# Additions of a tile and scatters of a step left unordered among themselves; the input's load taken in the preceding step, routing and norms spread over turns

## The chip, the core and the metric

The kernel runs on one core of a Trainium2 chip. The core has five engines that run side by side and wait for one another through semaphores: PE (TensorE, matrix products), DVE (VectorE), ACT (ScalarE), POOL (GpSimd) and SP (SyncE, which here only issues transfers). In the traces an engine starts its instructions in the order in which they stand in its stream, so one that waits holds up all behind it. Transfers are carried out by 16 DMA engines shared by all queues. The metric is device microseconds of the one core; lower is better.

## The reference, cut to what matters

Two layers work on an image batch x of 2 x 56 x 56 x 256 numbers in float32 (6272 tokens of 256 channels).

```python
# layer 0: neighborhood attention, window 7 x 7, 8 heads
x = x + L0_conv(_gn(x), ...)
# layer 1: linear attention with a gate and a running sum over tokens
t = x.reshape(B, 3136, 256)
t = t + L1_attn(_ln_t(t), ...)
# layer 1: a mixture of 8 experts, each token goes to its best two
probs = softmax(_ln_t(t) @ gate_w + gate_b)
top2_vals, top2_idx = top_k(probs, 2)
cw = zeros.at[token, top2_idx].add(top2_vals)
for e in range(8):
    t += cw[:, e] * (gelu(xf @ W1[e] + b1[e]) @ W2[e] + b2[e])
```

All of it is computed in float32. The attention of layer 1 carries sums from token to token, so it goes through the tokens in order. The experts need only a token's normalized value, its two experts and their weights.

## The kernel before, in words

**Layer 0** (up to about 485 us) is not touched by the change. It leaves its result in device memory (`x1_d`).

**Layer 1** is the function `layer_1`, run with `general` false. It cuts the tokens into 14 steps of 448 tokens (224 of each of the two images), held as four pieces of 112 tokens. The work of a step is written as Python generators that `yield` at the end of each turn:

- `before_pairs(s)` (from line 725) loads the step's input `x_acc` (line 729), normalizes and transposes it (`norm_T`, lines 690 to 722), projects it to q, k and v (line 749), and makes the gates and the softmax's running maxima and sums. Between norm and projection it adds the output bias `bo1` to x (line 737).
- `attention(s)` makes the running sums (`sums_plain`, lines 867 to 965) and adds the projected result to x (line 981).
- `route(s)` stores x into `out` (line 1151), normalizes and transposes it into `xs` (`norm_T` again), makes the gate's softmax, ranks the experts and gives each token its two slots (`rowi`, line 1249). It then writes each token's row twice into `xs_d`, a buffer in device memory that has a region for every expert: eight indirect transfers from POOL, one for each piece of 112 tokens and each of the two slots (the scatters, line 1253). `listed(s)` writes down which blocks of 256 slots are full by now.
- `experts()` goes through 56 tiles of 256 slots. `fetch` reads a tile's rows from `xs_d` into `xg` (line 1361) and the expert's weights into `wj` (line 1365), two tiles ahead of their use, both issued by SP. `gather` transposes `xg` on PE, `hidden` makes the first product and the gelu (lines 1389 and 1396), `results` reads the token numbers out of `xg` (`rows_e`, a cast on DVE, line 1404), starts `ye` from the second bias (ACT, line 1421), makes the second product (line 1426), adds it to `ye` (DVE, line 1433) and adds `ye` to the tokens' rows in `out`: one indirect transfer from POOL, with addition, for each half of 128 rows (the additions, line 1436).

`together` advances these generators side by side: `attention(s)` is the main one, and `route(s - 1)`, `before_pairs(s + 1)` and the tiles of experts get their turns in proportion. Each gets a stretch of the main one in which it is to run:

```python
with_it.append((route(s - 1), n_route, 0, 0.6))
with_it.append((before_pairs(s + 1), n_before, 0, 1))
with_it.append((tiles, n_tiles * per_tile + (begin > 0), 0.5 if begin else 0, 1))
```

The last four tiles sure to be full run beside `route` of the last step, and the other 14 alone at the end.

The order that is traced in this way is the priority of a scheduler, which then fixes the order of each engine's stream and places every wait. It works from the accesses to each buffer: two instructions that write the same buffer are ordered by a wait for the earlier one. `xs_d` and `out` are one buffer each to it, whatever rows an indirect transfer touches. So each scatter waits until the scatter before it has landed, each addition until the addition before it has landed, each read of `xs_d` (line 1361) until the last scatter traced before it has landed, and a scatter also until reads of `xs_d` traced before it are done.

Rows of a tile that no token fills come from `empty`, whose token number points behind the 6272 rows of `out`, into 128 rows that nobody reads.

Of the kernel before, what the change touches and what calls it, by code (L numbers as in the profile page):

```python
# [14 lines left out]
F32 = mybir.dt.float32  # L15
# [3 lines left out]
ALU = mybir.AluOpType  # L19
# [4 lines left out]
P = 128  # L24
NB = 2
IMG = 56
L = IMG * IMG
C = 256
# [12 lines left out]
TT = 112  # L41
BLK = 448
BT = BLK // NB
NST = L // BT
# [41 lines left out]
def constants():  # L86

    c = {}
    c["gavg"] = np.kron(np.eye(P // 8), np.full((8, 8), 1 / 8)).astype(np.float32)

    ind = np.zeros((P, NG, NB, 16), np.float32)
    for g in range(NG):
        for b in range(NB):
            for p in range(P):
                ind[p, g, b, b * NH + g * 4 + p // HD] = 1
    c["ind"] = ind.reshape(P, -1)
    c["rep"] = np.ascontiguousarray(ind.transpose(3, 1, 2, 0)).reshape(16, -1)
# [12 lines left out]

    e2 = np.repeat(e, 2).astype(np.float32)
    i2 = np.tile(np.arange(2), NE).astype(np.float32)
    cand = np.concatenate([(e2 - NE) * RG + i2 * SL, e2, i2, i2 + 1, np.arange(NX) + 1, e])
    c["cand"] = np.ascontiguousarray(np.broadcast_to(cand.astype(np.float32), (P, cand.size)))

    empty = np.zeros((P, ROW), np.float32)
    empty[:, TOK] = NB * L + np.arange(P)
    c["empty"] = np.tile(empty, (1, SL // P))
# [35 lines left out]
def hybrid_kernel(ctx: ExitStack, tc: tile.TileContext, t: dict, out: bass.AP):  # L154
# [7 lines left out]
    xs_d = dram.tile([NE * RG + SL, ROW], F32, name="xs_d")  # L162
    ident = const.tile([P, P], F32, name="ident")
    make_identity(nc, ident)

    def load(pool, name, shape, src, eng=None, dt=F32):
        dst = pool.tile(shape, dt, name=name)
# [469 lines left out]
    def layer_1(general):  # L637
        with (
# [51 lines left out]
            def norm_T(x, tag, pool, xn=None):  # L690

                st = p2.tile([TT, NTI, 6], F32, tag="lst", name="lst")
                mv = p2.tile([TT, NTI, 2], F32, tag="lmv", name="lmv")
                for i in range(NTI):
                    nc.vector.bn_stats(st[:, i, :], x[:, i, :])
                    nc.vector.bn_aggr(mv[:, i, :], st[:, i, :])
                rs = p2.tile([TT, NTI], F32, tag="lrs", name="lrs")
                nc.vector.tensor_scalar_add(rs, mv[:, :, 1], LN_EPS)
                nc.scalar.activation(rs, rs, AF.Sqrt)
                nc.vector.reciprocal(rs, rs)  # L700
                xT = pool.tile([P, NG, BLK], F32, tag=tag, name=tag)
                if xn is None:
                    xn = p1.tile([TT, NTI, C], F32, tag="xn", name="xn")
                yield
                for i in range(NTI):
                    nc.vector.tensor_scalar(  # L706
                        xn[:, i, :C],
                        x[:, i, :],
                        mv[:, i, 0:1],
                        rs[:, i : i + 1],  # L710
                        ALU.subtract,
                        ALU.mult,
                    )
                for g in range(NG):
                    pt = ps_m.tile([P, NTI, TT], F32, tag="mm", name="pt_x")
                    for i in range(NTI):
                        nc.tensor.transpose(  # L717
                            pt[:, i, :], xn[:, i, g * P : (g + 1) * P], ident[:TT, :TT]
                        )
                    nc.scalar.copy(xT[:, g, :], pt.rearrange("p i t -> p (i t)"))  # L720
                    yield
                return xT

            def before_pairs(s):
# [3 lines left out]
                for b in range(NB):  # L728
# [5 lines left out]
                    )  # L734
                yield
                xT = yield from norm_T(x, "xT_a", p1)
                nc.vector.tensor_tensor(
                    x, x, bo1.unsqueeze(1).to_broadcast([TT, NTI, C]), ALU.add
                )
# [27 lines left out]
                for g in range(NG):  # L767
                    ps = ps_m.tile([P, BLK], F32, tag="mm", name="p_u")
                    nc.tensor.matmul(
                        ps,  # L770
                        lhsT=wbd[:, g].rearrange("p h e -> p (h e)"),
                        rhs=v[:, g, :],
                        start=True,
                        stop=True,
                    )
                    nc.vector.tensor_tensor(pd[:, 3, g, :], ps, k[:, g, :], ALU.mult)
                    yield
                ps = ps_m.tile([P, BT], F32, tag="mm", name="p_sum")
                at = 0
                for g in range(NG):  # L780
# [186 lines left out]
            def attention(s):  # L967
                x, q, k, v, gl, cf = ready.pop(s)
                yield from (sums_general if general else sums_plain)(s, q, k, v, gl, cf)

                for i in range(NTI):
                    ps = ps_m.tile([TT, C], F32, tag="mm", name="p_out")
# [173 lines left out]
            def route(s):  # L1146
# [1 line left out]
                nonlocal n_prev, c_prev, at_prev  # L1148
                x = routed.pop(s)
                for b in range(NB):  # L1150
                    nc.gpsimd.dma_start(
                        out=out[b * L + s * BT : b * L + (s + 1) * BT].rearrange(
                            "(i p) e -> p i e", p=TT
                        ),
                        in_=x[:, b * 2 : (b + 1) * 2, :],
                    )
                xs = p3.tile([TT, NTI, ROW], F32, tag="xs", name="xs")
                nc.gpsimd.memset(xs[:, :, CWC + NE :], 0.0)
# [89 lines left out]
                rowi = p2.tile([TT, 2, NTI], I32, tag="rowi", name="rowi")  # L1248
                nc.vector.tensor_scalar_add(rowi, rows, float(NE * RG))
                yield  # L1250
                for i in range(NTI):
                    for c in range(2):
                        nc.gpsimd.indirect_dma_start(  # L1253
                            out=xs_d[:, :],
                            out_offset=bass.IndirectOffsetOnAxis(
                                ap=rowi[:, c, i : i + 1].bitcast(U32), axis=0
                            ),
                            in_=xs[:, i, :],
                            in_offset=None,
                        )  # L1260
                    yield
                listed(s)
                yield

# [77 lines left out]
            def fetch(j):  # L1342
# [18 lines left out]
                nc.sync.dma_start(  # L1361
                    out=xg, in_=xs_d[bass.ds(row, SL), :].rearrange("(u p) c -> p u c", p=P)
                )
                wj = p3.tile([P, NG * FF + NF * C + NF + C], F32, tag="wj", name="wj")
                nc.sync.dma_start(
                    out=wj, in_=t["we"][bass.ds(exp, 1)].rearrange("o p c -> (o p) c")
# [33 lines left out]
            def results(j, hT, xg, wj):  # L1400
# [18 lines left out]
                for u in range(SL // P):  # L1419
                    y = p6.tile([P, C], F32, tag="ye", name="ye")  # L1420
                    nc.scalar.activation(y, b2, AF.Copy, scale=cws[:, u : u + 1])  # L1421
                    ys.append(y)
                for u, y in enumerate(ys):
                    py = ps_h.tile([P, C], F32, tag="mm", name="p_y")
                    for f in range(NF):
# [10 lines left out]
                    nc.gpsimd.indirect_dma_start(  # L1436
                        out=out[:, :],
                        out_offset=bass.IndirectOffsetOnAxis(
                            ap=rows[:, u : u + 1].bitcast(U32), axis=0
# [2 lines left out]
                        in_offset=None,  # L1442
                        compute_op=ALU.add,
                    )
                    yield

            def experts():

# [39 lines left out]


            ready, routed, listed_at = {}, {}, {}  # L1490
            ahead = 1 if general else 2
            wait = 1 if general else 4
            tiles = experts()
            per_tile = NF + 1 + SL // P
            n_before = sum(1 for _ in before_pairs(0)) + 1
            n_step, n_route = 45, 13
            for s in range(NST):
                n_tiles = max(0, sure(s - 1) - wait) - max(0, sure(s - 2) - wait)
                begin = n_tiles and sure(s - 2) <= wait
                with_it = []  # L1500
                if s and not general:
                    with_it.append((route(s - 1), n_route, 0, 0.6))
                if s + 1 < NST:
# [88 lines left out]
```

## Time and profile before

| | |
|---|---|
| time, median of 3 runs | 1746.69 us (1733.62 to 1760.24) |
| span of the profiled execution | 1705.8 us |
| PE busy | 1400.5 us (82%) |
| DVE busy | 921.0 us (54%) |
| ACT busy | 703.9 us (41%) |
| POOL busy | 449.8 us (26%) |
| scatters (line 1253) | 112, 953 ns on POOL each, 2.6 us from issue to landing |
| additions (line 1436) | 112, 1585 ns on POOL each, 3.9 us from issue to landing |

The profile is of one execution; its span is shorter than the median time. PE is busy 82% of the span, but a matmul counts as busy from its start to its modelled end, and at a lower clock each takes longer. The stretches are: layer 0 to 485 us, steps without expert tiles to about 730 us, steps with them to about 1450 us, then tiles alone. In the views below, "who waited for whom" gives the total, the number of times and the longest wait; in a timeline, the columns are the start in us, the duration in us, engine, line, operation and tiles, and in square brackets the idle time before and what ended it.

### The profile page before, as it was taken

To read this page: it belongs to the slowest core of one execution; us is meant where nothing else is said; L and a number is where in the kernel's file an instruction comes from. 1 tells how busy PE (TensorE), PEld (TensorE's weight loads), DVE (VectorE), ACT (ScalarE), POOL (GpSimd) and SP (SyncE) were. 2 spreads that over 40 slices of the span, in tenths; PEclk is the share of its full clock that TensorE was granted. 3 is DMA by queue.
4 is the path that set the end of the run, shared out by engine and by line. 5 is a ranking of instruction groups with operands and counts; after the bars stand their busy time and mean duration, and the time that the engine had idled before them with its cause. 6 is when DMAs were issued, how large, how long until landed. Compare 5 with 4: busy or idle time off the path is not lost. (4 is left out here: it accounts for less than half of the span.)

```text
span 1705.8 us, 28462 instructions
## 1 busy us (share of the span) xinstructions
PE 1400.5 (82%) x10672; PEld 1022.5 (60%) x10672; DVE 921.0 (54%) x2731; ACT 703.9 (41%) x1261; POOL 449.8 (26%) x496
## 2 busy tenths in 40 slices
PE   0799999999577779679898988989898896677873
PEld 0467667778344545456666666666676675565763
DVE  3456556666457887655647665674766564111110
ACT  0234343444243445356554645555554443222221
POOL 2123333333200222113231323223232232322222
PEclk9999999999687899879898989999998898888887
DMA  7445455555200111153524253252434335575552
GB/s 234 127 148 163 151 157 173 150 152 168 83 0 22 45 35 35 39 186 84 147 71 133 73 141 111 71 148 72 140 82 118 108 84 154 139 208 141 162 154 27
DMA packets 110770, 197.66 MB, mean 116 GB/s; under 512 B 17667, under 2 KB 92275, under 8 KB 103445
## 3 DMA queue, kind: packets, MB, share of 16 engines
q1 hardware_dynamic: 74596, 135.60, 24.5%
q0 software_dynamic: 32560, 54.55, 14.5%
q10 hardware_dynamic: 3456, 5.51, 1.0%
q8 instruction: 88, 1.44, 0.4%
q14 instruction: 70, 0.57, 0.1%
HBM read 138.85 MB, written 56.73 MB: 115 GB/s over the span
## 5 line engine op out<-in xcount | busy, mean ns | idle before, releaser
L1436 POOL DMA_INDIRECT out<-ye,rows_e x112 | 177.5, 1585 | 495.2 <-DVE ye L1433 130.4
L1389 PE MATMUL p_h<-xT_g,wj 128*128 128x256 f32 x896 | 249.9, 416 | 23.3 <-ACT qh L887 14.0
L1426 PE MATMUL p_y<-wj,hT 128*128 128x256 f32 x896 | 234.5, 411 | 36.0 <-ACT hT L1396 36.0
L1426 PEld LDWEIGHTS p_y<-wj,hT 128*128 128x128 f32 x896 | 180.8, 207 | 78.4 <-ACT hT L1396 40.4
L1389 PEld LDWEIGHTS p_h<-xT_g,wj 128*128 128x128 f32 x896 | 179.0, 209 | 71.1 <-issue 30.8
L1253 POOL DMA_INDIRECT xs_d<-xs,rowi x112 | 106.8, 953 | 316.0 <-DMA xs_d<-xs,rowi 166.4
L501 ACT ACTIVATE ex<-ex 98x1024 f32<-98x1024 f32 x98 | 103.9, 1060 | 196.6 <-DVE ex L495 190.6
L1433 DVE SCALAR_TENSOR_TENSOR ye<-p_y,cws,ye 128x256 f32<-128x256 f32 x112 | 53.5, 478 | 183.0 <-PE p_y L1426 182.7
L1396 ACT ACTIVATE hT<-p_h,wj 128x256 f32<-128x256 f32 x224 | 102.0, 470 | 116.0 <-PE p_h L1389 114.8
L495 DVE TENSOR_TENSOR ex<-sc,bias 98x1024 f32<-98x1024 f32 x98 | 119.6, 1221 | 48.4 <-PE sc L486 42.6
L1421 ACT ACTIVATE ye<-wj,cws 128x256 f32<-128x256 f32 x112 | 54.4, 504 | 176.2 <-DVE own_e L1408 107.9
L510 PE MATMUL po<-vw,ex 98*64 98x33 f32 x3136 | 116.8, 227 | 9.8 <-DMA vw<-v_d 9.6
L510 PEld LDWEIGHTS po<-vw,ex 98*64 98x64 f32 x3136 | 104.3, 140 | 26.4 <-DMA vw<-v_d 12.0
L486 PEld LDWEIGHTS sc<-qb,kc 64*98 64x98 f32 x1568 | 91.1, 164 | 40.0 <-issue 25.9
L486 PE MATMUL sc<-qb,kc 64*98 64x128 f32 x1568 | 112.9, 282 | 1.1 <-DVE ex L495 1.1
L915 PE MATMUL sc<-qh,v 128*112 128x448 f32 x224 | 107.5, 566 | 0.0
L923 DVE TENSOR_TENSOR qv<-sc,upto 112x448 f32<-112x448 f32 x112 | 68.9, 617 | 64.4 <-PE sc L915 63.7
L1404 DVE CAST rows_e<-xg 128x2 int32<-128x2 f32 x56 | 9.0, 167 | 148.8 <-DMA xg<-xs_d 148.8
L313 POOL TENSOR_TENSOR xo<-xo,xq 128x256 f32<-128x256 f32 x49 | 35.5, 724 | 161.5 <-DVE xo L307 155.9
L1396 ACT ACT_TABLE_LOAD x44 | 56.5, 1283 | 44.1 <-PE p_h L1389 43.5
L717 PE MATMUL pt_x<-ident,xs 112*128 112x112 f32 x112 | 28.2, 354 | 53.6 <-DVE xs L706 53.6
L974 PE MATMUL p_out<-L_woT,q 128*112 128x256 f32 x224 | 60.7, 397 | 11.0 <-DVE q L964 11.0
(229 smaller groups left out, 2479.1 us busy)
## 6 DMA issues: line engine op xcount, KB each, us to landing
wj<-in_we SPq DMA_DIRECT2D x56, 1154.0 KB
vw<-v_d SPq DMA_DIRECT2D x196, 101.1 KB
xg<-xs_d SPq DMA_DIRECT2D x56, 272.0 KB
v_d<-values POOLq DMA_DIRECT2D x28, 231.0 KB, 3.8
xq<-in_x SPq DMA_DIRECT2D x98, 64.0 KB
q_d<-evq POOLq DMA_DIRECT2D x28, 224.0 KB, 3.2
qb<-q_d SPq DMA_DIRECT2D x56, 112.0 KB
x_d<-xo POOLq DMA_DIRECT2D x98, 64.0 KB, 3.3
```

The lines of the kernel that those rows point to most:

```text
L486: nc.tensor.matmul(sc[:KN, p, b, k], lhsT=keys(i, j, k, b, rows, g), rhs=qb[rows, g, :, b, j * QN : (j + 1) * QN], start=True, stop=True,)
L495: nc.vector.tensor_tensor(ex[:KN], sc[:KN].rearrange("n p b k h q -> n p b (k h q)"), tables[kind][:KN, g].unsqueeze(2).to_broadcast(wide) ...
L501: nc.scalar.activation(ex[:KN], ex[:KN], AF.Exp)
L510: nc.tensor.matmul(po[b * QN : (b + 1) * QN, hh, :], lhsT=ex[:KN, p, b, k, h, :], rhs=vw[:KN, b, k, hh * (HD + 1) : (hh + 1) * (HD + 1)], ...
L915: nc.tensor.matmul(sc, lhsT=vg[:, i * TT : (i + 1) * TT], rhs=qh[:, :, i * TT : (i + 1) * TT], start=True, stop=True,)
L923: nc.vector.tensor_tensor(qv, sc, upto.unsqueeze(1).to_broadcast([TT, 4, TT]), ALU.mult)
L974: nc.tensor.matmul(ps, lhsT=q[:, g, i * TT : (i + 1) * TT], rhs=wo1[:, g, :], start=g == 0, stop=g == NG - 1,)
L1253: nc.gpsimd.indirect_dma_start(out=xs_d[:, :], out_offset=bass.IndirectOffsetOnAxis(ap=rowi[:, c, i : i + 1].bitcast(U32), axis=0), in_=xs ...
L1389: nc.tensor.matmul(ph, lhsT=w1[:, k, f * P : (f + 1) * P], rhs=xT[:, k, :], start=k == 0, stop=k == NG - 1,)
L1396: nc.scalar.activation(hT[:, f, :], ph, AF.Gelu, bias=b1[:, f : f + 1])
L1426: nc.tensor.matmul(py, lhsT=hT[:, f, u * P : (u + 1) * P], rhs=w2[:, f, :], start=f == 0, stop=f == NF - 1,)
L1436: nc.gpsimd.indirect_dma_start(out=out[:, :], out_offset=bass.IndirectOffsetOnAxis(ap=rows[:, u : u + 1].bitcast(U32), axis=0), in_=y, in_ ...
```

## The change

It takes away the order among transfers that touch different rows, moves a load, and lets the generators hand over more often.

- The two additions of a tile touch different rows of `out` (an expert takes a token once), and the eight scatters of a step different rows of `xs_d` (a slot has one token). `apart` tells the scheduler that there is no dependence among them. What must stay ordered is then written by hand with `follow`: the first scatter of a step waits for all scatters of the step before, a tile's additions wait for both additions of the tile before and for the stores of x since, and a fetch of `xg` waits for all scatters of the last finished step.
- Two unordered additions must not meet in the rows behind the tokens, so these become 256 rows instead of 128, and `empty` numbers them all.
- `before_pairs(s + 2)` is begun, up to its first hand-over (its load), at the end of step s.
- `norm_T` hands over after each second piece, the addition of `bo1` comes after the projections and has a turn of its own, and `attention` has one more turn before its output projection.
- `route` runs from 0.08 to 0.48 of the step instead of from 0 to 0.6.

```diff
-    empty = np.zeros((P, ROW), np.float32)
-    empty[:, TOK] = NB * L + np.arange(P)
+    empty = np.zeros((P, SL // P, ROW), np.float32)
+    empty[:, :, TOK] = NB * L + np.arange(SL).reshape(-1, P).T
...
+    def apart(now, others, why):
+        for o in others:
+            tc.declare_no_dep(now.ins, o.ins, reason=why)
+    def follow(now, others, why):
+        for o in others:
+            tc.add_manual_dep(now.ins, o.ins.name, follows, reason=why)
...  norm_T
+                    if i % 2:
+                        yield
...  before_pairs: x + bo1 goes from behind norm_T to behind the projections, with a yield
...  attention
                 yield from (sums_general if general else sums_plain)(s, q, k, v, gl, cf)
+                yield
...  route
+                now = []
                 for i in range(NTI):
                     for c in range(2):
-                        nc.gpsimd.indirect_dma_start(
+                        d = nc.gpsimd.indirect_dma_start(
                             out=xs_d[:, :],
...
+                        apart(d, now, "a slot has one token")
+                        if not now:
+                            follow(d, scattered, "one step's slots, then the next one's")
+                        now.append(d)
                     yield
+                scattered[:] = now
...  fetch
+                follow(d, scattered, "slots filled so far")
...  results
-                    nc.gpsimd.indirect_dma_start(
+                    d = nc.gpsimd.indirect_dma_start(
                         out=out[:, :],
...
+                    apart(d, now, "an expert takes a token once")
+                    follow(d, added + stored, "the sums so far")
+                    now.append(d)
                     yield
+                added[:] = now
+                stored.clear()
...
-            n_before = sum(1 for _ in before_pairs(0)) + 1
-            n_step, n_route = 45, 13
+            n_before = sum(1 for _ in before_pairs(0))
+            coming = before_pairs(1)
+            next(coming)
+            n_step, n_route = 46, 15
...
-                    with_it.append((route(s - 1), n_route, 0, 0.6))
+                    with_it.append((route(s - 1), n_route, 0.08, 0.48))
                 if s + 1 < NST:
-                    with_it.append((before_pairs(s + 1), n_before, 0, 1))
+                    with_it.append((coming, n_before, 0, 1))
...
+                if s + 2 < NST:
+                    coming = before_pairs(s + 2)
+                    next(coming)
-            together((() if general else route(NST - 1), n_route), (tiles, wait * per_tile, 0, 2))
+            together((() if general else route(NST - 1), n_route), (tiles, wait * per_tile, 0, 2.2))
...
-    out = nc.dram_tensor("out_0", (NB * L + P, C), F32, kind="ExternalOutput").ap()
+    out = nc.dram_tensor("out_0", (NB * L + SL, C), F32, kind="ExternalOutput").ap()
```

More of the change, by code (lines that the diff above doesn't have):

```diff
@@ L114, in constants @@
     c["cand"] = np.ascontiguousarray(np.broadcast_to(cand.astype(np.float32), (P, cand.size)))
-    empty = np.zeros((P, ROW), np.float32)
-    empty[:, TOK] = NB * L + np.arange(P)
-    c["empty"] = np.tile(empty, (1, SL // P))
+    empty = np.zeros((P, SL // P, ROW), np.float32)
+    empty[:, :, TOK] = NB * L + np.arange(SL).reshape(-1, P).T
+    c["empty"] = empty.reshape(P, -1)
     tok = np.zeros((TT, NST, NTI), np.float32)
@@ L164, in hybrid_kernel @@
     make_identity(nc, ident)
+    follows = mybir.DependencyInfo(mybir.DependencyClass.Sync, mybir.DependencyReason.DATA)
+    def apart(now, others, why):
[4 more added lines that the diff above has]
+            tc.add_manual_dep(now.ins, o.ins.name, follows, reason=why)
     def load(pool, name, shape, src, eng=None, dt=F32):
@@ L736, in before_pairs @@
                 xT = yield from norm_T(x, "xT_a", p1)
-                nc.vector.tensor_tensor(
-                    x, x, bo1.unsqueeze(1).to_broadcast([TT, NTI, C]), ALU.add
-                )
                 q, k, v = (
@@ L777, in before_pairs @@
                     yield
+                nc.vector.tensor_tensor(
+                    x, x, bo1.unsqueeze(1).to_broadcast([TT, NTI, C]), ALU.add
+                )
+                yield
                 ps = ps_m.tile([P, BT], F32, tag="mm", name="p_sum")
@@ L969, in attention @@
                 yield from (sums_general if general else sums_plain)(s, q, k, v, gl, cf)
+                yield
                 for i in range(NTI):
@@ L1150, in route @@
                 for b in range(NB):
[L1151 to L1155, printed above, removed]
+                    stored.append(
+                        nc.gpsimd.dma_start(
+                            out=out[b * L + s * BT : b * L + (s + 1) * BT].rearrange(
+                                "(i p) e -> p i e", p=TT
+                            ),
+                            in_=x[:, b * 2 : (b + 1) * 2, :],
+                        )
                     )
@@ L1360, in fetch @@
                 xg = p3.tile([P, SL // P, ROW], F32, tag="xg", name="xg")
-                nc.sync.dma_start(
+                d = nc.sync.dma_start(
                     out=xg, in_=xs_d[bass.ds(row, SL), :].rearrange("(u p) c -> p u c", p=P)
                 )
+                follow(d, scattered, "slots filled so far")
                 wj = p3.tile([P, NG * FF + NF * C + NF + C], F32, tag="wj", name="wj")
@@ L1422, in results @@
                     ys.append(y)
+                now = []
                 for u, y in enumerate(ys):
@@ L1490, in layer_1 @@
             ready, routed, listed_at = {}, {}, {}
+            scattered, stored, added = [], [], []
             ahead = 1 if general else 2
```

## The prediction

> **What bounds the kernel now.** I read the busy times first, by stretch, then who waits for whom, then the timelines around the waits. Times by stretch (columns: us, busy us and number of instructions of each engine, granted PE clock, DMA share, GB/s):
>
> ```profile
> 485.00:773.00 288.00, 226.46 (x1326) 147.76 (x1326) 204.40 (x653) 122.83 (x209) 43.11 (x48) 0.86 0.17 55
> 773.00:1371.00 598.00, 542.54 (x3010) 393.03 (x3008) 370.89 (x1274) 320.72 (x539) 165.12 (x144) 0.93 0.39 106
> 1371.00:1480.00 109.00, 79.64 (x443) 63.51 (x442) 44.10 (x197) 34.52 (x64) 38.81 (x33) 0.89 0.43 112
> 1480.00:1706.00 226.00, 161.24 (x664) 134.10 (x664) 28.57 (x128) 55.09 (x126) 58.97 (x38) 0.84 0.54 147
> ```
>
> PE carries the most work in every stretch, yet stands idle for 61, 55, 29 and 65 us, and its clock is not the full one. No engine is the limit all along; what counts is what stops PE. Waits of the whole run:
>
> ```profile
> POOL xs_d L1253 <- DMA xs_d<-xs,rowi: 166.4, 77, 4.7
> ...
> DVE rows_e L1404 <- DMA xg<-xs_d: 148.8, 32, 18.7
> ...
> POOL out L1436 <- DMA out<-ye,rows_e: 115.1, 32, 6.6
> ```
>
> POOL waits scatter after scatter and addition after addition; DVE waits for a tile's rows. That these hang together shows in one step. POOL (start, us):
>
> ```profile
> 870.63 0.96 POOL L1253 DMA_INDIRECT xs_d<-xs,rowi  x1 [5.13 <-issue]
> 873.46 0.96 POOL L1253 DMA_INDIRECT xs_d<-xs,rowi  x1 [1.88 <-DMA xs_d<-xs,rowi]
> ...
> 893.96 0.94 POOL L1253 DMA_INDIRECT xs_d<-xs,rowi  x1 [3.30 <-DMA xs_d<-xs,rowi]
> ```
>
> Eight scatters take from 870.6 to 894.9 us. Then SP, DVE and PE:
>
> ```profile
> 896.60 0.41 SPq L1361 DMA_DIRECT2D xg<-xs_d  x1
> ...
> 899.32 0.17 DVE L1404 CAST rows_e<-xg 128x2 int32<-128x2 f32 x1 [7.41 <-DMA xg<-xs_d]
> ...
> 904.08 2.05 PE L1389 MATMUL p_h<-xT_g,wj 128*128 128x256 f32 x4 [4.35 <-ACT qh L887]
> ```
>
> The fetch goes out only after the last scatter has landed, the cast at the head of DVE's stream waits 7.41 us for it, the softmax's small operations stand behind the cast, ACT behind those, and PE runs dry for 4.35 us. Then it is slow: granted clock 0.53 from 902 to 916 us, and 1.00 after, so four matmuls that take 1.03 us elsewhere take 2.05. The same shows at every step, with waits of 5 to 8 us. A second stop is the start of a step: PE waits for `xs` of route's norm (53.6 us in all, 11 times).
>
> In the tail, tiles alone:
>
> ```profile
> 1594.19 1.55 POOL L1436 DMA_INDIRECT out<-ye,rows_e  x1 [4.88 <-DMA out<-ye,rows_e]
> 1598.77 1.55 POOL L1436 DMA_INDIRECT out<-ye,rows_e  x1 [3.03 <-DMA out<-ye,rows_e]
> 1606.67 1.55 POOL L1436 DMA_INDIRECT out<-ye,rows_e  x1 [6.35 <-DMA out<-ye,rows_e]
> ```
>
> Additions follow each other at 4.5 us, and at up to 7.9 where a weights load is under way. From 1512.0 to 1671.1 us there are 28 intervals: 5.7 us each, 11.4 a tile. PE needs 7.35 a tile at full clock (1578.79 to 1586.14: products, transposes, products). Hence POOL's chain sets the tail: `ye` has six buffers, ACT waits for one (51.3 us in all), gelu stands behind it, PE waits.
>
> **What the Trainium skill says.** "DMA: Bandwidth & Descriptors", Anatomy of one DMA, puts about 2.0 us of a transfer issued by POOL down as fixed, mostly the confirmation of the last write. The trace agrees: 2.6 us for a scatter, 3.9 for an addition, whatever the engine did before. The same page, Two DMAs through the same engine are not ordered, says that only a semaphore orders them, so without the waits they do overlap; the trace before has no such pair on `out`, so it is silent. Its section Issuing engines are not separate DMA queues says that all queues share 16 DMA engines; the 7 us additions beside weights loads agree. "TensorE: Matmul & The Clock Gate", Part 1, has PE at half clock after some 3.4 us of idleness; 0.53 after the gap of 4.35 us agrees. So an avoided gap saves more than itself.
>
> **The change, part by part.**
>
> *Scatters.* Behind each other they need 0.95 us and 0.30 us of issue (the gap shown where nothing is waited for). The last starts 7 x 1.25 = 8.8 us after the first and lands 2.6 later; with 0.4 for SP the fetch is out 11.8 us after the first scatter, not 26.0. In every second step a fetch still stands between the fourth and fifth scatter, and the fifth must wait for its read: 3 x 1.25 + 2.6 + 0.4 + 2.7 (962.3 to 965.0 us, fetch to cast) = 9.5, then 0.3 + 3 x 1.25 + 2.6 + 0.4: 16.6 us instead of 28.7. So rows come 12 to 14 us sooner, more than the 7.4 us of the wait.
>
> But the casts move too. In the built order of the changed kernel there stands, between `rowi` (which the scatters need) and the step's casts, DVE work of 5.3 us in one kind of step (11.1 before), of 5.8 and 8.5 in the other (6.9 and 24.8 before), summed from the mean durations of these lines. Before, 11.1 us of work took 22.1 us of time (869.8 to 891.9), so I double: DVE arrives at 10.6, at 11.6 and about 18.2 us. The rows are there at 0.8 + 11.8 + 2.7 = 15.3, at 3.3 + 9.5 = 12.8 and at 3.3 + 16.6 + 2.7 = 22.6 us, with the first scatter 0.8 and 3.3 us behind `rowi` as before. Waits left: 4.7, 1.2, 4.4, together 10.3 us for two steps; before 7.4 + 3.7 + 1.6 + 6.2 = 18.9. Nearly half goes, and waits under 5 us leave PE a gap too short to lose its clock.
>
> *Norms.* In the built order the pairs' norm for the next step lies a step ahead, behind the routing's ranks, so at a step's start only the four operations for `xs` are left before the transposes, and PE has three groups of products and the first scores ahead of them. The 2 to 7 us waits of `pt_x` should mostly go. `x + bo1` moves behind the projections, beside PE work; the same count of operations, nothing gained or lost. The load of x keeps its place in SP's stream: nothing. Two more turns and another share of the step cost no instruction.
>
> *Steps, summed.* 773 to 1371 us: 55 us idle, and 598 x 0.07 = 42 us of clock not granted, which overlaps with idleness; I count 25. Of these 80 us I take 35 back. 485 to 773: three `pt_x` waits (20.7), 15.2 + 4.4 at the first tile, which waits for the scatters' end, and clock; of some 50 I take 25. 1371 to 1480: 9.3 of `pt_x`, 16.0 for the rows behind the last scatters (1450.3 to 1475.5, of which some 12 go); 15. Together 75.
>
> *Additions.* A pair needs 1.55 + 0.3 to the second issue, 3.9 to its landing and 0.71 until the next starts: 6.5 us, below PE's 7.35. Bounds: with the longest landing (7.4) it is 10.0. A tile moves 1.15 MB of weights, 0.27 of rows and 0.26 of results; at the 236 GB/s that 1480 to 1530 us shows that is 7.1 us, so most pairs meet a load. I take 8.9 for the tile: a mean landing of 5.7, as the additions of 1541 and 1588 us had, makes 8.3, and something for alternation. 38 additions start after 1480 us, 19 tiles: 19 x (11.4 - 8.9) = 47 us. Waits added by `follow` are for transfers that were already waited for before; behind a waiting pair stand only later additions, scatters and the small memset, as now. The larger `empty` and `out` cost nothing: one load of the same size at the start.
>
> Sum 75 + 47 = 122: 1747 - 122 = 1625 us.
>
> **Rivals.** (a) *All stops go.* For it: rows come 12 to 14 us sooner, PE has work. Against: in-order streams find another wait. Steps would give 125 of 155 us, the tail at PE's 7.5 us 74: 1548. (b) *The casts take the gain.* Moved ahead, they wait as long as before, at another place; the steps give only the 15 us around the first and last scatters, and pairs beside loads take 9.8: 19 x 1.6 = 30. 1702. (c) *Slower.* The casts wait before the scores' masks and the `pd` products, so DVE blocks while PE has less in hand, and routing packed into 0.4 of a step holds back attention; PE then loses 8 us more in each of ten steps, clock included: +80 - 45 = 1782. For it: DVE is already 62% busy there. Against: the longest wait I find is 4.7 us. (d) *Additions are bound by the DMA engines*: pairs at 10.0 us with the steps as forecast: 1747 - 75 - 27 = 1645, within the main case.
>
> **Chances.** Main case (with d) 0.55, all stops go 0.22, casts 0.16, slower 0.07. A 2% change is 35 us, 1712 and 1782: faster 0.86 (the main case, a, and somewhat over half of b), same 0.09, slower 0.05 (c's upper half). The range 1555 to 1715 takes in the main case with both ends of the additions, most of (a) and most of (b).
>
> **What would show it.** Scatters 1.25 us apart; the fetch 12 to 17 us after the first; casts waiting under 5 us; `pt_x` hardly waiting for `xs`; the granted clock near 1 at step changes; additions in pairs 1.9 us apart, 8 to 9.5 us a pair after 1450 us; no ACT wait for an addition. Wrong, if casts wait 6 us and more right behind the listing, or a pair takes over 10 us.

## The result and the profile after

The changed kernel takes 1604.66 us (median of 4 runs, 1597.73 to 1616.02) where the kernel before took 1740.15 us beside it (4 runs, 1726.85 to 1760.24): a ratio of 0.925, with a 95% interval from 0.915 to 0.935. Forecast were 1625 us, between 1555 and 1715. Where a kernel below has no ratio, some of its executions were disturbed and none was worked out, and the ratios of e9, e10 and e11 rest on only four executions of the kernel before out of seven.

A single profile also contains layer 0, which the change does not touch, and which took 485.6 us in the profile before and 518.1 in the one after (more on that at the end). So I compare layer 1 alone, in three stretches that begin where PE forms `p_gt` of step 0, of step 5 and of step 13: the steps without expert tiles and the first tiles, then eight like steps with tiles, then the last step and the tiles alone.

| us in the profile | step 0 to 5 | 5 to 13 | 13 to end | layer 1 |
|---|---|---|---|---|
| before | 287.6 | 597.8 | 334.8 | 1220.2 |
| after | 276.9 | 567.0 | 252.2 | 1096.1 |
| difference | -10.7 | -30.8 | -82.6 | -124.1 |

The same stretches by engine, of the changed kernel (columns: us, busy us and number of instructions of PE, PE's weight loads, DVE, ACT and POOL, granted PE clock, DMA share, GB/s):

```profile
518.00:795.00 277.00, 231.82 (x1326) 147.97 (x1326) 201.42 (x646) 121.02 (x207) 45.53 (x49) 0.90 0.18 57
795.00:1362.00 567.00, 528.96 (x3009) 379.45 (x3008) 367.61 (x1267) 324.55 (x541) 162.42 (x144) 0.96 0.41 112
1362.00:1614.00 252.00, 221.15 (x1107) 186.14 (x1106) 73.77 (x326) 91.00 (x191) 97.94 (x72) 0.94 0.65 181
```

PE is now idle for 38 us of the middle stretch instead of 55, and for 31 of the last. The gain in the middle stretch lies in every second step only: steps 6, 8, 10 and 12 are 9 to 17 us shorter than before, steps 5, 7, 9 and 11 are 3 to 6 us longer.

The first stretch needs care. In steps 2 and 3 no expert tile runs yet, and the kernel e1 below has there the same instructions in the same order on every engine as the kernel before. Yet it takes 109.4 us for them at a granted clock of 0.81, and the kernel before 98.8 at 0.91. So a difference of 10.7 us over this stretch says little by itself. Step 4 alone, in which the first tiles wait for their rows, went from 92.6 to 83.2 us.

The waits of the whole run (total, number, longest):

```profile
DVE rows_e L1428 <- DMA xg<-xs_d: 130.8, 43, 8.6
...
POOL out L1461 <- DMA out<-ye,rows_e: 15.8, 3, 8.0
...
PE p_n L1235 <- DVE lrs L711: 11.1, 4, 4.5
PE p_n L1235 <- DVE taken L1231: 8.5, 8, 2.2
...
PE pt_x L730 <- DVE xs L717: 4.2, 4, 1.1
```

Three of the four kinds of stop are gone or small: POOL waits 15.8 us between additions instead of 115.1, no scatter waits for another any more, and `pt_x` waits 4.2 us for `xs` instead of 53.6 (in its place PE has new waits at `p_n`, the ranks of the routing). The fourth is as it was: the casts of `rows_e` wait 130.8 us, 148.8 before. In steps 5 to 13 alone these waits add up to 72.2 us after and 72.6 before. A step shows how that can be, although the rows come much sooner. First POOL:

```profile
892.24 0.99 POOL L1271 DMA_INDIRECT xs_d<-xs,rowi  x1 [5.22 <-issue]
893.53 0.96 POOL L1271 DMA_INDIRECT xs_d<-xs,rowi  x1 [0.30 <-issue]
...
900.99 0.94 POOL L1271 DMA_INDIRECT xs_d<-xs,rowi  x1 [0.30 <-issue]
```

Eight scatters in 9.7 us, none of them waiting for another. Then DVE, SP and PE:

```profile
897.70 0.68 DVE L907 TENSOR_TENSOR kt<-p_kt,glT 112x512 f32<-112x512 f32 x1
...
903.89 0.41 SPq L1384 DMA_DIRECT2D xg<-xs_d  x1
...
906.93 0.17 DVE L1428 CAST rows_e<-xg 128x2 int32<-128x2 f32 x1 [8.55 <-DMA xg<-xs_d]
...
907.74 2.07 PE L1413 MATMUL p_h<-xT_g,wj 128*128 128x256 f32 x4 [3.57 <-DVE pd L769]
```

The fetch goes out 11.7 us after the first scatter, as forecast. But DVE has done its last operation ahead of the cast at 898.4, 7.0 us after `rowi`, and stands for 8.55 us with the cast at the head of its stream. The `pd` product behind the cast is what PE waits for, 3.57 us, and the next four matmuls take 2.07 us instead of the 1.03 of others like them: half clock again.

In the tail (the tiles alone) POOL now issues pairs:

```profile
1550.51 1.55 POOL L1461 DMA_INDIRECT out<-ye,rows_e  x1 [3.65 <-DVE own_e L1432]
1552.37 1.56 POOL L1461 DMA_INDIRECT out<-ye,rows_e  x1 [0.30 <-issue]
1558.09 1.55 POOL L1461 DMA_INDIRECT out<-ye,rows_e  x1 [4.16 <-DVE own_e L1432]
1559.95 1.56 POOL L1461 DMA_INDIRECT out<-ye,rows_e  x1 [0.30 <-issue]
```

The second of a pair starts 1.86 us after the first, and what ends POOL's idleness is DVE's work on the next tile, no longer a transfer. From 1499.1 to 1594.2 us there are 13 tiles, 7.3 us each. PE hardly stops there and has its full clock:

```profile
1483.00:1603.00 120.00, 117.30 (x572) 102.90 (x570) 25.15 (x107) 49.22 (x109) 51.86 (x34) 1.00 0.75 205
```

### The profile page after: what moved, and what is told of

Read it like the earlier page. It is cut to its first block, busy times and chain, and to the rows that moved or that the text cites. A ratio compares the mean times of both kernels' runs of the same rounds, so it can differ in the third digit from the quotient of the medians.

```text
span 1614.2 us, 28500 instructions
## 1 busy us (share of the span) xinstructions
PE 1404.5 (87%) x10672; PEld 1028.5 (64%) x10672; DVE 918.9 (57%) x2731; ACT 707.9 (44%) x1265; POOL 449.9 (28%) x496
## 5 line engine op out<-in xcount | busy, mean ns | idle before, releaser
L1413 PE MATMUL p_h<-xT_g,wj 128*128 128x256 f32 x896 | 230.5, 395 | 15.1 <-DVE pd L769 10.8
L1451 PE MATMUL p_y<-wj,hT 128*128 128x256 f32 x896 | 220.8, 393 | 7.2 <-ACT hT L1420 7.1
L1413 PEld LDWEIGHTS p_h<-xT_g,wj 128*128 128x128 f32 x896 | 168.7, 196 | 56.2 <-issue 22.7
L1451 PEld LDWEIGHTS p_y<-wj,hT 128*128 128x128 f32 x896 | 171.4, 197 | 42.5 <-issue 11.6
L1271 POOL DMA_INDIRECT xs_d<-xs,rowi x112 | 107.2, 957 | 178.1 <-DVE hit L1338 71.8
L521 PE MATMUL po<-vw,ex 98*64 98x33 f32 x3136 | 130.9, 243 | 5.5 <-DMA vw<-v_d 5.5
L521 PEld LDWEIGHTS po<-vw,ex 98*64 98x64 f32 x3136 | 119.3, 160 | 23.5 <-DMA vw<-v_d 6.6
L497 PEld LDWEIGHTS sc<-qb,kc 64*98 64x98 f32 x1568 | 107.8, 190 | 39.5 <-issue 26.8
L497 PE MATMUL sc<-qb,kc 64*98 64x128 f32 x1568 | 132.3, 315 | 0.0
L1428 DVE CAST rows_e<-xg 128x2 int32<-128x2 f32 x56 | 9.5, 169 | 131.0 <-DMA xg<-xs_d 130.8
L446 ACT ACTIVATE kc<-pk,bk 128x112 f32<-128x112 f32 x196 | 50.6, 371 | 38.2 <-PE pk L415 38.2
L1167 POOL DMA_DIRECT2D out<-x_acc x28 | 20.4, 729 | 166.0 <-DVE x_acc L996 61.5
```

Of the source, the lines that this page charges most:

```text
L497: nc.tensor.matmul(sc[:KN, p, b, k], lhsT=keys(i, j, k, b, rows, g), rhs=qb[rows, g, :, b, j * QN : (j + 1) * QN], start=True, stop=True,)
L521: nc.tensor.matmul(po[b * QN : (b + 1) * QN, hh, :], lhsT=ex[:KN, p, b, k, h, :], rhs=vw[:KN, b, k, hh * (HD + 1) : (hh + 1) * (HD + 1)], ...
L1271: d = nc.gpsimd.indirect_dma_start(out=xs_d[:, :], out_offset=bass.IndirectOffsetOnAxis(ap=rowi[:, c, i : i + 1].bitcast(U32), axis=0), in ...
L1413: nc.tensor.matmul(ph, lhsT=w1[:, k, f * P : (f + 1) * P], rhs=xT[:, k, :], start=k == 0, stop=k == NG - 1,)
L1451: nc.tensor.matmul(py, lhsT=hT[:, f, u * P : (u + 1) * P], rhs=w2[:, f, :], start=f == 0, stop=f == NF - 1,)
```

## The experiments

Two questions: which part of the change brings how much, and why the casts wait as long as before. All ratios are to the kernel before on the same chip; the medians come from several chips. The stretches come from one profiled execution of each kernel. The last two columns are for steps 5 to 13: the waits of the casts, and PE's gaps of over 1.5 us, with the sum of each.

| kernel | us (median) | ratio, 95% interval | step 0 to 5 | 5 to 13 | 13 to end | cast waits | PE gaps |
|---|---|---|---|---|---|---|---|
| before | 1740.15 | 1 | 287.6 | 597.8 | 334.8 | 72.6 | 52.1 (14) |
| after | 1604.66 | 0.925 (0.915 to 0.935) | 276.9 | 567.0 | 252.2 | 72.2 | 35.0 (11) |
| e1 additions only | 1639.73 | 0.939 (0.934 to 0.943) | 300.0 | 585.6 | 263.3 | 54.3 | 43.0 (13) |
| e2 scatters only | 1704.25 | none | 285.2 | 567.2 | 332.4 | 60.3 | 33.2 (11) |
| e3 spreading only | 1722.51 | 0.985 (0.980 to 0.989) | 289.1 | 587.0 | 334.9 | 51.7 | 52.2 (11) |
| e4 after, late cast | 1565.81 | 0.897 (0.893 to 0.901) | 277.8 | 532.2 | 242.2 | 0 | 15.6 (4) |
| e5 before, late cast | 1673.36 | 0.955 (0.944 to 0.966) | 286.5 | 534.4 | 338.2 | 0 | 18.7 (7) |
| e6 after, scatters ordered | 1637.98 | 0.941 (0.934 to 0.948) | 283.4 | 566.5 | 263.4 | 56.5 | 37.4 (10) |
| e7 as e6, late cast | 1589.73 | none | 280.9 | 531.5 | 258.6 | 0 | 14.5 (4) |
| e8 without spreading | 1597.62 | 0.916 (0.909 to 0.924) | 273.8 | 557.2 | 252.7 | 71.8 | 26.0 (11) |
| e9 as e8, late cast | 1580.70 | 0.912 (0.900 to 0.925) | 283.4 | 536.4 | 243.8 | 0 | 18.7 (7) |
| e10 after, route 0 to 0.6 | 1591.76 | 0.917 (0.904 to 0.930) | 274.5 | 549.8 | 251.7 | 40.7 | 13.2 (4) |
| e11 after, additions ordered | 1703.87 | 0.985 (0.970 to 1.000) | 278.1 | 573.8 | 333.6 | 64.7 | 38.3 (11) |
| e12 e10 with late cast | 1557.17 | 0.893 (0.888 to 0.898) | 276.5 | 525.4 | 243.6 | 0 | 0 (0) |

### One part alone (e1, e2, e3)

e1 is the kernel before with the pairs of additions alone, and with what belongs to them (the 256 rows behind the tokens, the noted additions and stores):

```diff
+                now = []
...
-                    nc.gpsimd.indirect_dma_start(
+                    d = nc.gpsimd.indirect_dma_start(
                         out=out[:, :],
...
+                    apart(d, now, "an expert takes a token once")
+                    follow(d, added + stored, "the sums so far")
+                    now.append(d)
```

> The kernel before with the additions of a tile unordered, and nothing else of the change. Theory 1 (the additions give the tail alone, and there PE becomes the bound): a tile in the tail takes 7.4 us instead of 11.4, some 19 tiles, 70 to 80 us less than before, and the steps (773 to 1371 us before) keep their 598 us within 5. Theory 2 (the additions' chain also holds up POOL, and with it the steps): over 90 us less, with the steps shorter by 20 or more.

Measured: 1639.73 us, 108 less than the 1747.52 before beside it. Neither expectation holds: the total is that of theory 2, but the middle stretch is only 12 us shorter, and the last gives 71.5. By layer 1 in the profiles, e1 is 71.3 us shorter than the kernel before, of 124.1 for the whole change, or 83.7 of 113.4 without the first stretch. The rest of the 108 does not show in layer 1, the only part that the change touches, so I don't count it: layer 0 took 489.0 us in e1's profile and 506 to 523 in every other but that of the kernel before (the last section has more on that). The tail comes to within 11 us of the changed kernel's. Those 11 us are the rows behind the last scatters, for which PE waits 12.3 us here.

e2 takes the scatters alone, with the rule for the fetch:

```diff
+                        apart(d, now, "a slot has one token")
+                        if not now:
+                            follow(d, scattered, "one step's slots, then the next one's")
+                        now.append(d)
...
-                nc.sync.dma_start(
+                d = nc.sync.dma_start(
...
+                follow(d, scattered, "slots filled so far")
```

> The kernel before with the scatters of a step unordered, and nothing else of the change. Theory 1 (the casts in DVE's stream move ahead with the shorter chain and wait as long as before, so the steps gain nothing): 10 to 25 us less than before, all of it at the first tile and behind the last scatters; cast waits of about 8 us stay in every step. Theory 2 (rows that come 12 to 14 us sooner free the steps): 40 to 60 us less, cast waits under 5 us.

Measured: 1684.68 to 1713.54 us against 1747.52, so 34 to 63 less. The middle stretch falls from 597.8 to 567.2, while the casts still wait 60.3 us. Neither theory holds: the steps gain, though the casts go on waiting. The last stretch stays, 332.4: rows that come sooner are worth nothing there while the additions' chain sets the pace.

e3 takes the moved load, the turns and the shares of the step alone:

```diff
-                    with_it.append((route(s - 1), n_route, 0, 0.6))
+                    with_it.append((route(s - 1), n_route, 0.08, 0.48))
...
-                    with_it.append((before_pairs(s + 1), n_before, 0, 1))
+                    with_it.append((coming, n_before, 0, 1))
```

> The kernel before with the norms and routing spread over turns, the load moved and bo1 moved, but with additions and scatters ordered as before. Theory 1 (the spreading is what shortens the steps): PE's waits for the norm at the start of a step go (53.6 us before, under 10 here), 30 to 45 us less than before. Theory 2 (the steps gain from the scatters): 0 to 15 us less.

Measured: 1722.51 us, ratio 0.985: 25 us less, between the two expectations. The middle stretch falls by 10.8 us, all of layer 1 by 9.2. The waits of the whole run:

```profile
DVE rows_e L1418 <- DMA xg<-xs_d: 125.0, 26, 20.7
...
PE p_n L1232 <- DVE lrs L710: 19.7, 4, 7.0
PE p_n L1232 <- DVE taken L1228: 15.3, 8, 3.9
...
PE pt_x L729 <- DVE xs L716: 7.6, 4, 4.9
```

The waits of `pt_x` go, 53.6 to 7.6 us, and 35 us of new ones at `p_n` come: in the denser routing PE reaches the ranks before DVE has them. One wait is swapped for another.

### The cast at the head of DVE's stream (e4, e5, e6, e7)

If the cast only stands too early in DVE's order, nothing but its place has to change. In e4 it stays behind the weights `own_e` of its tile by a dependence without a semaphore:

```diff
-                nc.vector.tensor_copy(rows, xg[:, :, TOK : TOK + 1].rearrange("p u o -> p (u o)"))
...
+                cast = nc.vector.tensor_copy(
+                    rows, xg[:, :, TOK : TOK + 1].rearrange("p u o -> p (u o)")
+                )
+                tc.add_manual_dep(cast.ins, last.ins.name, behind_own, reason="the weights first")
```

> The changed kernel with the cast of a tile's token numbers kept behind the weighting of the same tile in DVE's stream (an edge of order alone, no further wait). Theory 1 (the cast at the head of DVE's stream is what still stops PE in the steps): DVE's waits for rows fall from 131 us to under 40, PE's gaps of 3 to 4 us before the hidden products and the sums go, and the time is 20 to 40 us below the changed kernel's 1605, about 1570. Theory 2 (the wait only moves to the next reader of the rows, the transposes on PE or the weighting): within 10 us of 1605.

Measured: 1565.81 us, ratio 0.897. DVE in one step:

```profile
890.59 0.23 DVE L1434 SCALAR_TENSOR_TENSOR own_e<-cand,l_exp,xg 128x8 f32<-128x8 f32 x1
...
891.42 0.17 DVE L1443 CAST rows_e<-xg 128x2 int32<-128x2 f32 x1
891.49 0.62 DVE L789 TENSOR_TENSOR pd<-p_u,k 128x448 f32<-128x448 f32 x1
```

No bracket: neither `own_e` nor the cast waits, since DVE comes to them when the rows have arrived. In steps 5 to 13 the streams of all five engines stand in the same order as in the changed kernel but for the casts, so nothing else that moved can be the cause. The middle stretch takes 532.2 us, PE is granted 0.98 of its clock:

```profile
784.00:1316.00 532.00, 514.45 (x3007) 373.28 (x3006) 370.39 (x1268) 324.47 (x542) 162.16 (x143) 0.98 0.44 119
```

e5 makes the same edit in the kernel before, with every order kept.

> The kernel before, with nothing of the change, but with the cast of a tile's token numbers kept behind the weighting of the same tile in DVE's stream. Theory 1 (the scatter chain stops the steps through the cast alone): DVE's waits for rows in the steps go, the steps fall from 598 to under 575 us, and 25 to 45 us are saved in all; the waits of 15 us at the first tile and behind the last scatters stay. Theory 2 (rows are late for their other readers too): the waits move to the transposes on PE or the weighting, under 10 us saved.

Measured: 1673.36 us, ratio 0.955, and 534.4 us in the middle stretch. The cast moved in each tile is worth 63 us there, twice what the whole change brings to that stretch, and more than theory 1 gave. Here too only the casts stand elsewhere in the streams of steps 5 to 13. The waits at the first tile (15.4 us) and behind the last scatters (16.2 us) stay.

e6 is the changed kernel with the scatters in order again, which removes the lines shown under e2.

> The changed kernel with its scatters ordered again; additions unordered and norms spread. Theory 1 (with the norms spread the scatters' order still costs the waits behind the first and last scatters and little in the steps): 20 to 30 us above 1605, of it 10 in the steps. Theory 2 (scatters carry most of the steps' gain also beside the other parts): 35 us and more above, with over 20 in the steps.

Measured: 1637.98 us, ratio 0.941, between the two expectations. The middle stretch is that of the changed kernel, 566.5 and 567.0, so the 10 us of theory 1 are not there; what comes back lies at its two ends. PE:

```profile
765.06 1.11 PE L1391 MATMUL pt_g<-ident,xg 128*128 128x128 f32 x4 [18.45 <-DMA xg<-xs_d]
...
1480.70 1.08 PE L1391 MATMUL pt_g<-ident,xg 128*128 128x128 f32 x4 [12.05 <-DMA xg<-xs_d]
```

At the first tile PE waits 18.45 us instead of 7.9, and 12.05 us behind the last scatters, where it does not stop at all in the changed kernel. Beside both other parts, then, unordered scatters bring the middle steps nothing: the scatters take longer in e6, yet its casts wait less (56.5 us), because they stand later in the stream. In every second step 34 instructions of DVE stand between `rowi` and the waiting cast, where the changed kernel has 17, and the casts are all that stands elsewhere in DVE's stream in the middle steps.

e7 has both edits, e4's and e6's.

> The kernel with the late cast (1566 us) with its scatters ordered again. Theory 1 (in the steps the scatters' chain works through the cast alone): the steps keep their 532 us within 8, and the 15 to 25 us that come on top lie at the first tile and behind the last scatters: about 1587. Theory 2 (the chain also stops the steps in other ways): steps over 550 us, 1610 and more.

Measured: 1589.73 us in the median, from 1559.77 to 1594.39. With no ratio I lean on it only for the middle stretch: 531.5 us with ordered scatters, as with unordered ones.

### Spreading beside the other parts (e8, e9, e10, e12)

e8 is the changed kernel without e3's lines.

> The kernel before with additions and scatters unordered, and without the spreading of norms and routing. Theory 1 (the spreading adds little once scatters are unordered, since the casts then wait earlier and longer in its denser routing): 1605 within 12. Theory 2 (its 25 us come on top): 1630 and more.

Measured: 1597.62 us, ratio 0.916, whose interval overlaps the changed kernel's. The middle stretch is 10 us shorter, 557.2. Spreading, worth 25 us alone by the total, is worth nothing here, as theory 1 had it. It and the unordered scatters cover for each other: beside the additions (e1, 585.6 us) either brings the middle stretch down, the scatters to 557.2 (e8), the spreading to 566.5 (e6), and both together to 567.0.

e9 adds the late cast to e8.

> Additions and scatters without order, the cast behind the weights of its tile (own_e), and no spreading of norms and routing. Theory 1 (the cast's place in DVE's stream is the block of the middle steps, whatever else is changed): steps 5 to 13 take 528 to 536 us as with the late cast beside all parts (532), the tail 240 to 250, in all 1555 to 1580. Theory 2 (with the cast out of the way the spreading does its own work, because the waits of route's transposes for xs come back without it): those waits are there again with 40 us or more, steps 540 to 555, in all 1580 to 1605.

Measured: 1580.70 us and 536.4 in the middle, at the edge between the two expectations; the waits of `pt_x` for `xs` are back at 39.2 us. With the cast out of the way spreading is worth 4 us of the middle stretch (532.2 in e4), too little to lean on, and the intervals of the two ratios just overlap.

e10 puts one number of the changed kernel back:

```diff
-                    with_it.append((route(s - 1), n_route, 0.08, 0.48))
+                    with_it.append((route(s - 1), n_route, 0, 0.6))
```

> The changed kernel with one number put back: the routing spread over 0 to 0.6 of a step, not 0.08 to 0.48. Theory 1 (the 10 us that the steps 5 to 13 take more with the spreading than without, 567 against 557, come from the denser routing): steps 555 to 560, in all 1590 to 1600. Theory 2 (they come from the norm a step ahead and the casts' new places, not from the share): steps 563 to 570, in all 1600 to 1612, and the waits of the casts 18 to 19 us per two steps as before.

Measured: 1591.76 us, within theory 1, and 549.8 in the middle, below both expectations. The denser routing is what cost time there: at 0 to 0.6 there is no `p_n` wait in the middle steps, and the casts wait 40.7 us instead of 72.2. By total time the two kernels can't be told apart (the intervals overlap); by stretch and by waits they can.

e12 joins e10 and e4.

> The changed kernel with both: the cast behind the weights of its tile, and the routing spread over 0 to 0.6 of a step. Theory 1 (the denser routing costs PE time of its own, the 3.5 to 4.3 us waits of p_n in every second step that were left beside the late cast): these waits go, steps 5 to 13 take 515 to 526 us, in all 1548 to 1562. Theory 2 (the denser routing costs only by where it puts the cast, so that with the late cast nothing is left to gain): steps 529 to 535, in all 1563 to 1573.

Measured: 1557.17 us (6 runs), ratio 0.893: faster than both kernels, and by its median the fastest tried; against e4 the intervals overlap. The middle stretch is at the edge of what theory 1 gave, 525.4 us, with no PE gap over 1.5 us:

```profile
790.00:1315.00 525.00, 516.03 (x3006) 372.69 (x3005) 370.32 (x1274) 326.87 (x543) 162.69 (x143) 0.99 0.44 121
```

PE is busy for 516 of 525 us at 0.99 of its clock, so no more than 9 us of idleness are left to take out of these steps. Against e9 (536.4) the spreading with the wider routing is worth 11 us of them.

### The additions taken back (e11)

The changed kernel without the lines shown under e1:

> The changed kernel with its additions in order again, everything else kept. Theory 1 (the additions' chain alone sets the tail): the time from step 13 to the end goes from 252 back to 325 to 335 us, ACT waits for a free ye again (40 us or more), steps 5 to 13 stay at 562 to 572, in all 1675 to 1695. Theory 2 (part of the tail's gain is the earlier rows behind the last scatters): tail 310 to 322, in all 1655 to 1672.

Measured: 1703.87 us, ratio 0.985. The last stretch is 333.6 us again, as theory 1 had it; the total is higher than either theory gave: the middle steps lose 7 us too, and for the rest I have no account. Waits of the whole run:

```profile
POOL out L1457 <- DMA out<-ye,rows_e: 112.9, 26, 7.6
...
ACT ye L1442 <- DMA out<-ye,rows_e: 77.4, 19, 6.1
```

ACT waits for a free `ye` again, with unordered scatters and early rows in place. From 1501.9 to 1666.8 us a tile takes 11.8 us. With e1 this shows both ways that the additions' order set the tail.

## Why the prediction was right, and where it was not

The time was right because the sum was: 122 us forecast, 124.1 in layer 1 of the two profiles. That the sum came so close is luck. The first two stretches gave 41.5 us where 60 were forecast, the last 82.6 where 62 were, and the errors cancel.

- **Additions, forecast 47 us.** Right in mechanism, too small: the mis-sized term is the 8.9 us a tile. It is 7.3, and 19 x (11.4 - 7.3) = 78 us; e1 gives 71.5 in the last stretch, e11 takes back 81.4. I let most pairs meet a weights load and take longer than PE's 7.35. Three times POOL still waits for the pair before: at 1457.9 and 1466.2 us, 11.4 and 8.3 us after the start of that pair, and once at the very end. From 1473 to 1594 us it never does: what ends POOL's idleness is DVE, which waits for PE. So there the rival with pairs at 10 us falls, although 205 GB/s and a DMA share of 0.75 are more than before. Its bound of 10 was read too low, all the same: the longest landing in the tail before is 9.5 us (the addition of 1501.69), not 7.4, and the 11.4 us of one pair show that such a pair can occur. On the Trainium skill's "DMA: Bandwidth & Descriptors", Two DMAs through the same engine are not ordered, the trace before was silent. Now the second addition starts 1.86 us after the first, while an addition of the tail before took at least 3.5 us to land, so they overlap by this estimate; the trace after doesn't give their landings. The page's Rules for kernel authors also say that an accumulating transfer beside another access of the same bytes can lose an addition; that is what `follow` keeps apart, and no run here tries it.
- **Scatters.** Right: 1.25 us apart, the fetch 11.7 us after the first (forecast 11.8), and 15.4 to 17.1 in every second step (16.6), where the fifth scatter still waits for a read. Worth: 11 us at the first tile (step 4 takes 94.4 us in e6 and 83.2 in the changed kernel) and 11 in the last stretch, where I had put 25 and 15 together with `pt_x`; in between nothing once additions and spreading are in, 28 us (585.6 to 557.2) where only the additions are.
- **Casts: the step that failed.** "DVE arrives at 10.6" after "so I double": 5.3 us of DVE work took 7.0 us of time, not 10.6, while the rows came at 15.5 us, as forecast (15.3). In the other kind of step it arrived at 8.1 to 8.7 and 13.8 to 14.4 us, not at 11.6 and 18.2. The factor of 2 came from a stretch with waits in it; of the 7.0 us only 2.0 are idle. So "nearly half goes" is wrong: 72.2 us of waits against 72.6 in these eight steps, where 41 were forecast (10.3 for each two steps). This is rival (b), to which I gave 0.16, as far as the casts go; its figures fell, since the steps gave more than its 15 us and the last stretch 82.6 instead of 30. The sign that I named for a wrong forecast, casts that wait 6 us and more right behind the listing, is there.
- **Steps, forecast 25 + 35 + 15.** Measured: 10.7 in the first stretch, of which 9.4 lie in step 4, and 30.8 in the second; the third can't be split from the additions, though e11, with all but the additions, is at 333.6 against 334.8, so there the 15 were worth nothing until the additions' chain was gone. The 35 came out nearly right for another reason than mine. The waits of PE for `xs` in these steps went from 24.9 us to nearly nothing and 13.2 came at `p_n`; 11.3 us of waits of `p_gt` for `x_acc` went as well; and PE's clock rose from 0.93 to 0.96.
- **Norms.** The `pt_x` waits went, as forecast. It is true that another share of the step cost no instruction, and yet it cost time: 567.0 against 549.8 us (e10). I had named it in rival (c) and valued it only there.
- **Clock.** "Near 1 at step changes" failed with the casts: it comes to 0.98 and 0.99 in e4 and e12, where few gaps or none are left. The Trainium skill's "TensorE: Matmul & The Clock Gate", Part 1, fits: the gap of 3.57 us above, at the edge of the 3.4 us that the page gives, is followed by half clock.

Why does a cast wait the same whether its rows come early or late? The experiments show that its place decides: moved alone, it takes 63 us out of the middle of the kernel before and 35 out of the changed one's, and with it late the stretch is 525 to 536 us under every mix of the other parts tried. The scheduler puts it earlier when the scatters' order is dropped: e6 and the changed kernel differ in nothing but that order and the fetch's rule, and the cast stands behind 34 instructions in one and behind 17 in the other. That it does so because it believes the rows to come earlier fits, but its reckoning was not tested. The sum of cast waits alone does not give the time either (71.8 us in e8 at 557.2, 51.7 in e3 at 587.0). I take it that what counts is how much work PE has in hand while DVE stands; no run isolates that.

## What to carry to other kernels

Dropping an order among transfers pays where the chain itself is what ends last, as with the additions: check what the next bound is, and take its time as the new pace where nothing measured speaks against it (PE's 7.35 us here; I had put a guess about contention on top). Where a transfer's reader waits at the head of an in-order engine, look at where that reader stands before shortening the transfer: the cast moved behind its neighbours did more for the middle steps (63 us in e5) than eight overlapped scatters (31 in e2). And measure the parts together: in the middle steps they gave 12, 31 and 11 us alone and 31 together, and spreading was worth nothing beside the two others.

## What the runs showed of the hardware

PE's clock can stay at half for long while PE has work. In the profile of the changed kernel this lay in layer 0, which no kernel here touches:

```profile
391.00:497.00 106.00, 88.79 (x1090) 79.24 (x1091) 44.64 (x95) 24.95 (x26) 26.87 (x42) 0.50 0.34 99
```

106 us at 0.50 with PE busy for 84% of them; the rest is one gap of 17.2 us, which ended at 493.4. Ahead of the stretch the longest gap in 15 us is 1.31 us. The matmuls bear the clock out: from 395 to 475 us, with PE never idle, the products `sc` of layer 0 take 417 ns in the median, and 269 from 300 to 390. In the profile before, the same loop ran at full clock from 395 to 437 us. What sets the half clock off I do not know. It goes with the length of layer 0: the mean clock of the layer is 0.95 where it took 485.6 us (before) and 489.0 (e1), and 0.87 to 0.90 where it took 506 to 523 (all others). That is more than some of the edits are worth, which is why the stretches of layer 1 are compared here.
